# Moving weight packing, a slot table and an exponential to other steps of a two-layer graph kernel

## The chip, the core and the metric

The kernel runs on one core of a Trainium2 chip. A core has a matrix engine (TensorE, PE in the profile; PEld is its weight load), a vector engine (VectorE, DVE), a scalar engine for activations (ScalarE, ACT), a general engine (GpSimd, POOL) and a queue engine that only starts transfers (SyncE, SP). Each works through its own instructions in order, and they wait for each other by semaphores. Sixteen DMA engines carry the transfers that SP, ACT and POOL start. The metric is the device time of one execution in microseconds, and of several executions the median.

## The reference

Two layers follow each other on x of 2708 rows and 256 columns, with a 0/1 matrix adj of 2708 by 2708. Each layer is an attention over the graph and a mixture of eight experts of which each row uses two.

```python
# layer 0
x = x + elu(softmax(where(adj > 0, q @ k.T / 16, -9e15)) @ v)      # q, k, v from layernorm(x)
x = x + ffn0(layernorm(x))      # top 2 of 8 experts, 256 -> 1024 -> 256, gelu, own layer norm
# layer 1
x = x + softmax(where(A > 0, s_src + s_dst + b, -1e9)) @ H         # H = layernorm(x) @ W_fc + b_fc
x = x + ffn1(layernorm(x))      # top 2 of 8 experts, 256 -> 512 -> 256, gelu
```

## The kernel before

**Stages.** Attention of layer 0, expert stage of layer 0, attention of layer 1, expert stage of layer 1, and a last sum. The change touches the first of these and, through what it takes away from it, the second.

**Attention of layer 0** (`layer0_attention`). The queries are cut into six blocks: five of 512 rows and a last one of 148 (`BLOCKS`; `last` is 5). For each block a loop runs over 22 tiles of 128 keys (`for k in range(NT)`); a pass through it is called a key step here. A key step multiplies keys with queries (`scores`, L568), takes the exponential on ScalarE (L580), multiplies by the mask on VectorE (L583), and, three steps later (`LAG`), multiplies the result with the values (`attend`, L632). Score results lie in two buffers of PSUM (`ps_s`). In block 0 the rows of x are also normalised and turned (`prepare`), four tiles ahead of their use.

**Masks.** The mask of a block is made in the block before it (`masks_of`, one step per key step from key 2), from 1 MB pieces of adj that SP loads into three buffers. The first block's own mask is made beside it. When a block is done, its mask is stored in DRAM (L741), since layer 1 uses it again; six entries at the end of the background list load the masks back into SBUF (`mT<-neighbours`).

**Background list.** `background` is a list of transfers that depend on nothing in the kernel: 2 fills of scratch rows (`disp<-nobody`), then 32 pieces that copy expert weights of layer 0 from their places in DRAM into one packed row per partition (`pack_weights`, pieces of 512 KB and a few small ones, L1067 to L1085), then 16 entries of two 256 KB pieces each for layer 1, and, from the end of the attention on, the 6 loads of masks. One entry is taken in every second key step of the attention, from key 11 of block 1 on, and none in the last block: 39 in all. What remains is taken in the expert stage, one in every second slot (L1616).

**What follows a block.** When a block's last key has been attended, its up to four accumulators are copied out (`evict`, L657), and each tile of 128 rows gets a generator `finish`. `line` starts these generators with a gap of so many key steps (3, in the last block 4) and moves every running one by a step in each key step (`line.step()`), from block 1 on. A step ends at a `yield`. The first step of `finish` divides by the row sum and takes the negative part (L644) and its exponential (L645); the second forms the elu and adds x; then `experts0.route` normalises the row, finds the two best experts (L1243 to L1259), takes an exponential for their weights (L1261), counts with two small matmuls (L1264, L1265) and scatters the row by an indirect transfer into the rows of its experts (L1282). The first 16 tiles find the logits by dot products on VectorE (L261), the others by a matmul (L1232).

**The slot table.** The expert stage works in slots of 128 rows of one expert. Weights of a slot lie in one of four ring buffers. The first 24 slots are worked out during the last block, from the first 16 tiles, by `place(0, 24)`: a small matmul for the counts (L1303), and some twenty VectorE instructions (L1305 to L1394), with four `yield`s in between. `begin_steps` puts a `yield` before it, then fetches rows for three slots (`fetch_rows`, SP: four transfers of 32 KB and one small one each, L1465 and L1471), then weights for three slots (`fetch_weights`, POOL, L1446), each with a `yield`. The ring's first three buffers are filled by a guess beforehand (L1441, three loads of 2182 KB).

**Order.** SP's order is the order of the program in the whole kernel. In blocks 0 to 4 the other engines' instructions are ordered by a planner when the kernel is built, with the program's order as priority. From the last block on the order of PE, ACT and DVE is also the program's (`order0`); POOL's isn't.

**Expert stage of layer 0** (`slots`). A slot takes 48 recorded matmuls in two parts (`up`, L1533, and `down`, L1549) with a gelu between them (L1541); the next slot's rows are turned and scaled on VectorE (L1506, L1512), which reads the slot's weights from its ring buffer. Two `line.step()` per slot finish the last tiles' routes. When they are done, or at slot 21, the remaining slots are placed.

Of the kernel before, what the change touches and what calls it, by code (L numbers as in the profile page):

```python
# [77 lines left out]
LAG = 3  # L78
# [26 lines left out]
def adj_ffn_kernel(ctx: ExitStack, tc: tile.TileContext, a: dict, out: bass.AP):  # L105
# [208 lines left out]
    def over_sum(raw, r, n, total, alone):  # L314

        z = small.tile([P, 2], F32, name="z")
        nc.vector.tensor_scalar(alone, raw[:r, n : n + 1], 0.0, None, ALU.is_equal)
        nc.vector.scalar_tensor_tensor(
            z[:r, 0:1], alone, float(N), raw[:r, n : n + 1], op0=ALU.mult, op1=ALU.add
        )  # L320
        nc.vector.reciprocal(z[:r, 1:2], z[:r, 0:1])
        nc.vector.scalar_tensor_tensor(
            raw[:r, :n], total[:r], alone, raw[:r, :n], op0=ALU.mult, op1=ALU.add
        )
        return z[:r, 1:2]
# [47 lines left out]
    def layer0_attention(line):  # L373
        with ExitStack() as scope, ExitStack() as until_last:

            last = len(BLOCKS) - 1
# [18 lines left out]
            def load_x(t):  # L395
                xin[t] = rows0.tile([P, D], F32, name="xin", bufs=9)
                nc.sync.dma_start(xin[t][: ROWS[t]], of_tile(a["x"], t))
# [60 lines left out]
            def mask_of(b):  # L458
                mT = of_block(b, "mT", [P, MASKS[b].width], FP8, bufs=3)
                nc.gpsimd.memset(MASKS[b].of_key(mT, NT - 1).bitcast(F32), 0.0)  # L460
                return mT

            def norm_begin(t):
                r, src = ROWS[t], xin.pop(t)
                return t, src, norm_stats(src[:r], r)

            def norm_end(t, src, stats):
                r, (mean, factor, *_) = ROWS[t], stats
                xn = rows.tile([P, D], F32, name="xn", bufs=4)
                normed(xn[:r], src[:r], mean, factor)  # L470
                return xn

            def prepare(t, xn):
                r = ROWS[t]
                at = xnT[:, :, t * P : t * P + r]
                if t < NT - 1:
                    to_columns(at, xn[:r], r)
                else:
                    tail_columns(x_tail, xn)
                    nc.vector.tensor_copy(at, x_tail[:, :, :r])  # L480
                    r, at = P, x_tail
                nc.vector.tensor_reduce(
                    sums_of[:, :, t], xnT[:, :, t * P : t * P + ROWS[t]], AX.X, ALU.add
                )
                ps = misc.tile([P, GROUP, P], F32, name="misc").rearrange("p g n -> p (g n)")
                for c in range(DC):
                    nc.tensor.matmul(
                        ps[:r, :D], at[:, c, :], wv[:, c, :],
                        start=(c == 0), stop=(c == DC - 1),
                    )  # L490
                nc.scalar.copy(v[:r, t, :D], ps[:r, :D])
# [145 lines left out]
            def finish(t, raw, total):  # L637
                r, xr = ROWS[t], xin.pop(t)
                rinv = over_sum(raw, r, D, total, alone[:r, t : t + 1])
                nc.vector.scalar_tensor_tensor(  # L640
                    raw[:r, :D], raw[:r, :D], rinv, bv_b[:r], op0=ALU.mult, op1=ALU.add
                )
                neg = rows0.tile([P, D], F32, name="neg", bufs=2)
                nc.vector.tensor_scalar(neg[:r], raw[:r, :D], 0.0, None, ALU.min)  # L644
                nc.scalar.activation(neg[:r], neg[:r], AF.Exp)  # L645
                yield
                nc.vector.scalar_tensor_tensor(
                    neg[:r], neg[:r], -1.0, raw[:r, :D], op0=ALU.add, op1=ALU.max
                )
                x1 = rows0.tile([P, D], F32, name="x1")  # L650
                nc.vector.tensor_add(x1[:r], neg[:r], xr[:r])
                yield from experts0.route(t, x1)
# [14 lines left out]
            for b, (b0, nb, ts_) in enumerate(BLOCKS):  # L667
                later_mask = iter(())
                if b == last:
                    line.gap = GROUP  # L670
                    order0.enter_context(
                        tc.manual_schedule(engines={
                            mybir.EngineType.PE,
                            mybir.EngineType.Activation,
                            mybir.EngineType.DVE,
                        })
                    )
                if b + 1 < len(BLOCKS):
                    mT_next = mask_of(b + 1)
                    later_mask = masks_of(b + 1, mT_next)  # L680
                for k in range(NT):
                    if b == 0:
                        if k + 9 < NT:
                            load_x(k + 9)
                        next(first_mask, None)
                        if k + 4 < NT:
                            prepare(k + 4, norm_end(*norm_begin(k + 4)))

                    j = k - (2 if b == last else NT - 1 - GROUP)
                    if 0 <= j < len(ts_):  # L690
                        load_x(ts_[j])
                    if k == (0 if b == last else GROUP):
                        apart_adj = load_apart(b)
                    if k == NT - 8:
                        apart = compare_apart(*apart_adj)
                    late.append((b, k, scores(b, k, g, apart, mT)))
                    if len(late) > LAG:
                        b_, k_, p = late.pop(0)
                        if k_ == 0:
                            accs = [  # L700
                                ps_acc.tile([P, D + 1], F32, name="acc") for _ in BLOCKS[b_][2]
                            ]
                        attend(b_, k_, p, accs)
                        if k_ == NT - 1:
                            evict(b_, accs, total)
                    if b == 1 and k % GROUP == 0:
                        next(folding, None)
                    if b == 0 and k == NT - 1:
                        sums = wide.tile([P, DC], F32, name="sums", bufs=1)
                        nc.vector.tensor_reduce(sums, sums_of, AX.X, ALU.add)  # L710
                        total = all_sum(wide, sums, wv, D, "total0")
                    if b == 0 and k == NT - 4:
                        raw = wide.tile([P, BN // QUARTER, P], I32, name="adj", bufs=3)
                        raw = raw.rearrange("p n e -> p (n e)").bitcast(F32)
                        nc.sync.dma_start(
                            raw, a["L0_ffn_Wr"].rearrange("d e -> (d e)").partition_broadcast(P)
                        )
                        gate_rows(raw)
                    if k == NT - 6 and b + 1 < len(BLOCKS):
                        g_next = queries(b + 1)  # L720
                    if k >= 2:
                        next(later_mask, None)
                    if background and k % 2 == 1 and b < last and (b > 1 or (b == 1 and k > 10)):
                        background.pop(0)()
                    if b > 0:
                        line.step()
                    if b == last and k == LAG:
                        until_last.close()
                    if b == last and k == LAG + 2:
                        n = FULL_AFTER[experts0.early]  # L730
                        guess0 = experts0.open(
                            [i * (n // RING) * E // (n + GROUP) for i in range(AHEAD)] + [-1]
                        )
                        for _ in range(AHEAD):
                            next(guess0)
                        begin0 = experts0.begin()
                        for _ in range(6):
                            next(begin0)
                    if b == last and k in (LAG + 7, LAG + 11, LAG + 15):
                        next(begin0)  # L740
                nc.sync.dma_start(neighbours[b][:], mT)  # L741
                if b < last:
                    for _ in later_mask:
                        pass
                    g, mT = g_next, mT_next
# [903 lines left out]
    background = []  # L1649
# [92 lines left out]
```

## Time and profile before

Three executions took 1217.05 us in the median (1210.39 to 1219.58). The profiled execution took 1209.07 us; its span, from first to last instruction, is 1206.8 us, with a mean granted TensorE clock of 0.981.

| engine | busy us | share of the span | instructions |
|---|---|---|---|
| VectorE | 621.0 | 51% | 2389 |
| ScalarE | 422.9 | 35% | 1234 |
| GpSimd | 419.9 | 35% | 524 |

| stretch | us |
|---|---|
| blocks 1 to 4 of the first attention | 81.5, 82.7, 79.6, 78.5 |
| last block (148 queries) | 54.2 |
| first expert stage | 332.9 |

Block starts are the starts of the first score matmul (L568) of a block. The page cuts the span into 40 slices of 30 us and gives the busy share of each engine in tenths, then the granted clock and the mean share of the DMA engines. A long busy share says which engine is in demand; where that engine idles, the instruction behind the gap says what it waited for. In the timeline each line is a start, a duration, the engine, the source line, the operation, what it writes and reads, and in brackets how long the engine had been idle and what ended that.

### The profile page before, as it was taken

What the parts mean: (1) busy time and instruction counts of PE and PEld (TensorE: products, weight loads), DVE (VectorE), ACT (ScalarE), POOL (GpSimd) and SP (SyncE); (2) the same over time, 40 slices, a digit from 0 to 9 for tenths busy, and PEclk for the clock granted to TensorE, in tenths of its full rate; (3) what the DMA queues carried; (4) which work ended last, traced back from release to release, by engine and by line L of the source; (5) the groups of instructions that cost most, each with busy time, mean ns of one, the idle gap of its engine ahead of it and who ended that gap; (6) DMA issues with size and microseconds to landing.
All of it is one profiled execution on the core that took longest, in us unless ns stands there. A gap on an engine that the chain in (4) does not pass through costs nothing. (4 is left out here: it accounts for less than half of the span.)

```text
span 1206.8 us, 20877 instructions
## 1 busy us (share of the span) xinstructions
PE 1131.4 (94%) x6416; PEld 914.3 (76%) x6416; DVE 621.0 (51%) x2389; ACT 422.9 (35%) x1234; POOL 419.9 (35%) x524
## 2 busy tenths in 40 slices
PE   8989999999999998899999999998999998999990
PEld 5666666656666664699989989996999977899880
DVE  5465992865856747652222222224866777322214
ACT  3222221212122121443333323333776657544430
POOL 3011220120220303244333234433745557655540
PEclk9999999999999998999999999999999999999995
DMA  9293864976683389367868968634001527655557
GB/s 221 42 195 91 195 158 124 237 177 136 163 214 101 97 205 364 79 169 183 212 182 234 375 172 252 175 105 105 1 2 54 202 61 209 180 157 145 147 167 284
DMA packets 200717, 198.16 MB, mean 164 GB/s; under 512 B 92363, under 2 KB 183972, under 8 KB 194328
## 3 DMA queue, kind: packets, MB, share of 16 engines
q1 hardware_dynamic: 173530, 117.14, 39.6%
q0 software_dynamic: 26176, 76.85, 20.1%
q10 hardware_dynamic: 894, 2.77, 0.6%
q8 instruction: 53, 0.87, 0.3%
q14 instruction: 64, 0.52, 0.1%
HBM read 260.37 MB, written 66.15 MB: 271 GB/s over the span
## 5 line engine op out<-in xcount | busy, mean ns | idle before, releaser
L1533 PEld LDWEIGHTS mm<-xe,ring 128*128 128x128 f32 x2192 | 259.1, 193 | 25.4 <-DVE xe L1512 7.8
L1533 PE MATMUL mm<-xe,ring 128*128 128x128 f32 x2192 | 262.9, 277 | 16.3 <-DMA ring<-L_ffn_packed,weight_row 7.7
L1549 PE MATMUL acc<-ring,hT 128*128 128x256 f32 x1096 | 253.8, 382 | 0.7 <-ACT hT L1541 0.7
L1541 ACT ACTIVATE hT<-mm,ring 128x128 f32<-128x128 f32 x548 | 155.8, 369 | 273.2 <-PE mm L1533 139.4
L1549 PEld LDWEIGHTS acc<-ring,hT 128*128 128x128 f32 x1096 | 202.8, 192 | 25.0 <-ACT hT L1541 0.9
L632 PEld LDWEIGHTS acc<-v,p 128*128 128x128 f32 (+1 forms) x880 | 160.0, 190 | 63.4 <-issue 37.5
L568 PE MATMUL s<-g,xnT 128*128 128x512 f32 x420 | 202.3, 601 | 3.3 <-ACT p L580 3.3
L632 PE MATMUL acc<-v,p 128*128 128x257 f32 (+1 forms) x880 | 204.2, 384 | 0.6 <-DVE p L583 0.6
L1555 DVE SCALAR_TENSOR_TENSOR y<-acc,who,bias 128x256 f32<-128x256 f32 x92 | 44.4, 482 | 267.3 <-PE acc L1549 264.6
L277 POOL TENSOR_TENSOR ln_rs<-ln_rs,minus_half 128x2 f32<-128x2 f32 x88 | 66.1, 754 | 233.0 <-DVE ln_rs L273 210.0
L1282 POOL DMA_INDIRECT disp<-row,to x88 | 89.0, 1012 | 153.8 <-DVE to L1279 33.5
L1446 POOL DMA_INDIRECT ring<-L_ffn_packed,weight_row x92 | 97.5, 1059 | 107.7 <-PE acc L1549 68.5
L901 PE MATMUL acc<-parts,m 128*128 128x266 f32 x924 | 127.6, 296 | 0.0
L580 ACT ACTIVATE p<-s 128x512 f32<-128x512 f32 x105 | 62.0, 594 | 179.0 <-PE s L568 149.9
L901 PEld LDWEIGHTS acc<-parts,m 128*128 128x128 f32 x924 | 118.3, 187 | 4.4 <-ACT raw L928 0.9
L568 PEld LDWEIGHTS s<-g,xnT 128*128 128x128 f32 x420 | 77.3, 191 | 56.1 <-issue 48.2
L1568 POOL DMA_INDIRECT xd<-y,who x45 | 70.9, 1575 | 140.2 <-issue 71.3
L583 DVE SCALAR_TENSOR_TENSOR p<-p,mT 128x512 f32<-128x512 f32 x100 | 72.3, 725 | 58.3 <-ACT p L580 58.1
L868 ACT CAST m<-mT 128x512 fp32r<-128x512 fp8e4 (+4 forms) x168 | 72.2, 475 | 11.0 <-PE acc L901 7.6
L1512 DVE TENSOR_SCALAR xe<-xe_raw,ring 128x128 f32<-128x128 f32 x90 | 28.0, 360 | 65.7 <-DMA ring<-L_ffn_packed,weight_row 64.6
L1561 POOL DMA_INDIRECT xd<-y,who x47 | 46.9, 998 | 26.0 <-DVE y L1555 13.3
L261 DVE SCALAR_TENSOR_TENSOR row<-x,wr_rows 128x256 f32<-128x256 f32 x128 | 53.0, 416 | 0.3
(257 smaller groups left out, 1051.5 us busy)
## 6 DMA issues: line engine op xcount, KB each, us to landing
adj<-in_adj_dram SPq DMA_DIRECT2D x100, 256.0 KB
L_ffn_packed<-in_L_ffn_W_dram SPq DMA_DIRECT2D x32, 512.0 KB
xg<-disp SPq DMA_DIRECT2D x368, 32.0 KB
L_ffn_packed<-in_L_ffn_W_dram SPq DMA_DIRECT2D x32, 256.0 KB
neighbours<-mT SPq DMA_DIRECT2D x5, 1408.0 KB
mT<-neighbours SPq DMA_DIRECT2D x5, 1408.0 KB
ring<-L_ffn_packed SPq DMA_DIRECT2D x3, 2182.0 KB
xin<-in_x_dram SPq DMA_DIRECT2D x42, 128.0 KB
```

The costliest lines, as they stand in the source:

```text
L277: nc.gpsimd.tensor_tensor(rs[:r, 1], rs[:r, 0], minus_half[:r], ALU.pow)
L568: nc.tensor.matmul(ps[:kr, :nb], xnT[:, c, k0 : k0 + kr], g[:, c, :nb], start=(c == 0), stop=(c == DC - 1 and k < KEYS),)
L583: nc.vector.scalar_tensor_tensor(p, p, LARGEST, mask, op0=ALU.min, op1=ALU.mult)
L632: nc.tensor.matmul(accs[j][:r], p[keys, q0 : q0 + r], v[keys, k, :], start=(k == 0), stop=(k == NT - 1),)
L868: nc.scalar.copy(m[:, : q1 - q0], MASKS[b].of_key(mTs[b], k)[:, q0 - b * BN : q1 - b * BN],)
L901: nc.tensor.matmul(acc[:r], masks[t], parts[:, k, i], start=(k == 0 and i == 0), stop=False,)
L1282: nc.gpsimd.indirect_dma_start(disp[:], bass.IndirectOffsetOnAxis(ap=to[:r, j : j + 1], axis=0), rows2[:r, j], None,)
L1446: nc.gpsimd.indirect_dma_start(w, None, packed[:], bass.IndirectOffsetOnAxis(ap=self.weight_row[:, s : s + 1], axis=0), bounds_check=E * P ...
L1533: nc.tensor.matmul(ps[:, i, :], w[:, c * hidden + f * P : c * hidden + (f + 1) * P], xe[:, c, :], start=(c == 0), stop=(c == DC - 1),)
L1541: nc.scalar.activation(hT[:, f, :], ps[:, i, :], AF.Gelu, bias=w[:, b1 + f : b1 + f + 1])
L1549: nc.tensor.matmul(ps, hT[:, f, :], w[:, w2 + f * D : w2 + (f + 1) * D], start=(f == 0), stop=(f == hc - 1),)
L1568: start = nc.gpsimd.indirect_dma_start(xd[:], at, y, None, bounds_check=N - 1, oob_is_err=False, compute_op=ALU.add)
```

## The change

Three places in `layer0_attention`:

```diff
@@ finish @@
                 nc.vector.tensor_scalar(neg[:r], raw[:r, :D], 0.0, None, ALU.min)
+                yield
                 nc.scalar.activation(neg[:r], neg[:r], AF.Exp)
                 yield
@@ the loop over keys @@
-                    if background and k % 2 == 1 and b < last and (b > 1 or (b == 1 and k > 10)):
+                    if background and k % 2 == 1 and b < last and (b > 0 or k > 8):
                         background.pop(0)()
...
                         begin0 = experts0.begin()
-                        for _ in range(6):
-                            next(begin0)
-                    if b == last and k in (LAG + 7, LAG + 11, LAG + 15):
+                    if b == last and LAG + 2 <= k < LAG + 8:
+                        next(begin0)
+                    if b == last and k in (LAG + 9, LAG + 12, LAG + 15):
                         next(begin0)
```

The exponential of the negative part becomes a step of its own, one key step behind the instruction that forms the negative part; all later steps of a tile move by one. The background list is drawn on from key 9 of block 0 instead of key 11 of block 1: 51 places in the attention instead of 39, for 50 entries. In the last block the six steps that work out the slot table and fetch its rows, all taken at key 5 before, are taken one each at keys 5 to 10 (the first of them only reaches the first `yield`), and the three weight fetches at keys 12, 15 and 18 instead of 10, 14 and 18. No computation is added or left out.

## The prediction

> **What bounds the kernel now.** I read the page's shares first, then busy time by stretch (the six attention blocks by the starts of their score matmuls, and the first expert stage), then TensorE's waits in each stretch, and last the order in time around the long waits.
>
> ```profile
> PE 1131.4 (94%) x6416; PEld 914.3 (76%) x6416; DVE 621.0 (51%) x2389; ACT 422.9 (35%) x1234; POOL 419.9 (35%) x524
> ...
> 284.80:364.40 79.60, 78.48 (x302) 50.43 (x301) 53.43 (x225) 17.10 (x38) 13.24 (x19) 1.00 0.79 191
> 364.40:442.90 78.50, 77.50 (x306) 50.85 (x305) 52.47 (x219) 16.97 (x38) 16.27 (x25) 1.00 0.53 127
> 442.90:497.10 54.20, 46.48 (x242) 27.80 (x240) 35.13 (x152) 10.90 (x42) 14.61 (x26) 0.94 0.78 272
> 497.10:830.00 332.90, 325.68 (x2204) 304.03 (x2205) 96.43 (x306) 110.36 (x373) 122.02 (x96) 1.00 0.69 190
> ```
>
> Columns: stretch, length, then busy us of PE, weight load, DVE, ACT, POOL, the granted clock, DMA share, GB/s. TensorE leads everywhere, so a microsecond is won only where it idles or runs at a lower clock. Blocks 3 and 4 idle 1.1 and 1.0 us. The last block idles 7.7 of 54.2 us at a mean clock of 0.94: the change's main place. The first expert stage idles 7.2 us in 333.
>
> ```profile
> 458.92 0.61 PE L632 MATMUL acc<-v,p_last 128*20 128x257 f32 x2
> ...
> 460.60 0.18 DVE L1369 CAST token_row<-row 128x24 int32<-128x24 f32 x1
> ...
> 461.57 0.30 DVE L583 SCALAR_TENSOR_TENSOR p_last<-p_last,mT_last 128x148 f32<-128x148 f32 x1
> ...
> 463.60 0.42 ACT L645 ACTIVATE neg<-neg 128x256 f32<-128x256 f32 x1 [7.26 <-DVE neg L644]
> 463.92 0.46 ACT L580 ACTIVATE p_last<-s 128x148 f32<-128x148 f32 x2
> ...
> 464.25 1.35 PE L568 MATMUL s<-g_last,xnT 128*128 128x148 f32 x4 [4.72 <-ACT p_last L580]
> ```
>
> This is the long wait. The slot table's DVE chain (L1305 to L1394) runs from 457.04 to 461.65 in one piece; behind it come a mask product and the next tile's first part, ending in L644 at 463.56; ScalarE holds L645 at its head until then, and two score exponentials behind it; TensorE needs one of them to free a score buffer. It stands 4.72 us.
>
> ```profile
> 256.90 3.55 PE L568 MATMUL s<-g,xnT 128*128 128x512 f32 x4 [2.20 <-ACT p L580]
> ...
> 324.32 1.99 PE L568 MATMUL s<-g,xnT 128*128 128x512 f32 x4 [1.12 <-ACT p L580]
> ...
> PE mm L1533 <- DVE xe L1512: 5.7, 4, 2.6
> ...
> 698.72 0.60 DVE L1512 TENSOR_SCALAR xe<-xe_raw,ring 128x128 f32<-128x128 f32 x2 [7.98 <-DMA ring<-L_ffn_packed,weight_row]
> 699.12 3.87 PE L1533 MATMUL mm<-xe,ring 128*128 128x128 f32 x32 [2.62 <-DVE xe L1512]
> ```
>
> The other losses: two ScalarE-caused waits in blocks 2 and 3, and in the first expert stage four waits (1.11 at 509, 1.43 at 611, 0.53 at 682, 2.62 at 699; 5.7 in all), three of them on expert weights still in transfer.
>
> **What the Trainium skill says.** "TensorE: Matmul & The Clock Gate", What's actually happening: an idle array drops to half clock after about 3.4 us and needs as long a busy stretch to recover. The trace agrees on half speed (four 128x148 score matmuls take 1.35 us behind the stall, 0.75 to 0.77 elsewhere), but shows it already after 2.20 us (3.55 us against 1.88). "DMA: Bandwidth & Descriptors", Issuing engines are not separate DMA queues: transfers from SP and POOL share 16 engines and interleave. That agrees with weight fetches (POOL) arriving late just when SP's mask loads ran: 375 GB/s in that slice of the page. "Perfetto Trace Analysis", Sequencer Loop: an instruction waits for its semaphores in its engine's order; L645 above is that case.
>
> **Part 1: the table in five key steps.** Nothing is removed: 4.6 us of DVE work (457.04 to 461.65) falls into about 0.2, 1.6, 0.75, 1.45 and 0.55 us at keys 6 to 10 of the last block. PE's key step takes 1.7 us (472.07, 473.73, 475.47). Worth at most: the stall 4.72, and the slow clock behind it, where key steps took 3.19 and 2.59 us instead of 1.7 and 2.0: 2.1. Together 6.8.
>
> But DVE is next. I lined up its work by key from the durations of its rows: mask product 0.33; a tile's first part 1.8 (461.80 to 463.56), second 1.8 (465.42 to 467.23), normalising 1.1, top two 1.05, last part 0.9. Keys 5 to 12 then ask about 20 us of DVE against 14 us of PE, and the backlog that the three keys between score and product allow is used up near key 14. From there PE is paced by the exponentials behind tile 19's L644 (mine: about 478 instead of 481.35) and by its normalised row (about 484 instead of 486.6). I put the last score group at 484.5 instead of 488.97: **4.5 us**. Ends: 2 if the DVE pace is worse by one tile part, 6.8 if it hides.
>
> The row fetches move from key 5 to key 10 with the table: three times five SP transfers (L1465, L1471), now behind one more tile's store. SP waits there for token_row (about 466 instead of 460.8). Cover: three ring loads of 2182 KB issued at 457.04 block SP anyway: four row transfers from 465.06 took 18.32 us, to 483.4. First use is near 492, so nothing; without that cover some 6 us later, which would still land before 492. The weight fetches (POOL, 1.06 us each to issue) at keys 12, 15, 18 instead of 10, 14, 18 get their table some 8 us later, near 469.5; the fourth slot needs its weights only 21 us after the stage begins: nothing.
>
> **Part 2: the exponential a step later.** One ScalarE instruction of 0.42 us a tile, 22 of them, not removed. ScalarE idled 53.3 us before it on L644, but PE lost only the 1.12 us at 324 (and the stall above): **1.1 us**. The 2.20 at 256.90, plus 1.85 at half clock (3.55+2.08 against 1.88+1.90), belongs to another exponential (L1261, behind L1249), which isn't moved; I leave it. Each route ends a step later; at three steps between tiles DVE sees the same work, otherwise interleaved. In blocks 1 to 4 the order isn't written out by hand, so this is unknown: from +4.05 (the L1261 event goes) to -4.05 (another one appears) per block. I take nought. In the first expert stage DVE's 3.41 us wait before L647 at 504.54 goes, as its instruction now stands behind the next slot's input; with it the 1.11 at 509.
>
> **Part 3: packing from key 9 of block 0.** 7 entries come into block 0 (two fills of 129 KB, five of 512 KB) and 5 into block 1; all others move forward by 12, so all 50 are out before the last block. SP issues some 11 more transfers of 0.5 to 0.6 us in block 0, about 6 us. Cover: own masks and input rows are issued by key 12, packing of weights begins at key 13; DMA is 0.48, 0.73, 0.38 and 0.00 busy in the ten-us slices from 80 to 120. The gate's 1 MB load (SP at 104.29) is read by DVE only at 120.4. Block 1 gets the density of blocks 2 and 3, which idle little. Nothing; without the cover, up to 4 us at the start of block 1 (one half-clock event).
>
> The first expert stage loses eleven entries (SP at 513 to 651), and six mask loads move from slots 23 to 33 (SP at 666 to 742) to slots 1 to 11. The waits at 611, 682 and 699 sat under this traffic; without it, slots after 745 show none. Worth 4.6. Mask loads now meet the weight fetches of the first slots (249 GB/s at 540 to 555, where a packing entry is replaced by 1408 KB): I give back 2.2 of 4.6, close to the largest single wait, and take **2.4**; bounds -3 (all 5.7 again with more) to 4.6.
>
> **Sum.** 4.5 + 1.1 + 1.1 + 2.4 = 9.1 us. The profiled execution took 1209.07 us (span 1206.8 and 2.27 around it), so 1200 of its kind. It lies 8 us below the median of the runs; subtracted from 1217.05 it gives **1208 us**.
>
> **Rivals.** (a) *More is won*: DVE's backlog hides (6.8), the expert stage keeps 4.6 and the event at 256.9 goes (4.05): 6.8+2.2+4.6+4.05 = 17.7, 1199 us. For: ScalarE no longer waits at every tile. Against: 29.45 us DVE busy in the 38 us from 452 to 490. 30%. (b) *Nothing is won*: DVE's total is unchanged, so spreading only splits the stall, and the mask loads give their waits back: gains of 2 at most, 1215. 15%. (c) *Slower*: in blocks 1 to 4 the later exponential lengthens each route, DVE (13 to 14 of 15 us in stretches of blocks 2 and 3) delays L1249 or L644 more, and the event of 256.90 repeats, at 2.20 + 1.85 = 4.05 each. From three new ones the gain is gone; two in each of four blocks (32.4) less 9.1 give 1240, five give 1217 + 20.3 - 9.1 = 1228. Against: ScalarE's slack grows by a step. 12%. A change that doesn't do what it says is excluded by the code.
>
> **Numbers.** My forecast 43%. Its own range is 1202 to 1213; with (a), (b) and part of (c) 1197 to 1221. A change within 1% (12.2 us) is about what cannot be told from none: the three runs spread over 9.2 us. Faster by over 1%: all of (a) and a little of the forecast, 0.33; slower: most of (c), 0.11; same: 0.56.
>
> **What would show it.** Part 1 is right if the table's groups lie between other DVE work, the 4.72 disappears, the clock of the last block returns to 1.0, and its length falls to about 49.7. It is wrong if a wait of over 3 us on a ScalarE exponential stands in keys 9 to 18. Part 2: waits of L645 on L644 fall from 53.3 to under 20 us. Part 3: block 0 and 1 as long as before, no packing after the last block begins, no wait near the turn of the slots' second half; wrong if the first expert stage is longer. The forecast as a whole falls if blocks 1 to 4 (322.3 us) change by over 5 us.

## The result and the profile after

The change made the kernel slower: 1226.11 us in the median of seven executions (1223.01 to 1230.34) against 1217.05 (1210.39 to 1219.58), also of seven, a ratio of 1.0085 with a 95% interval of 1.0057 to 1.0114 (the two medians alone give 1.0074). The profiled execution of the changed kernel took 1230.34 us (span 1228.6), the longest of its seven; that of the kernel before took 1209.07 us and lies 8 us below its median. So the two traces differ by 21 us where the medians differ by 9, and the readings below rest on differences that come back in further traces.

In the changed kernel lines from 645 on carry a number higher by one: the exponential is L646, the mask store L742, the packing L1068 to L1086, the ring loads L1442, the row fetches L1466.

The busy times of the page, then the stretches from the first score matmul of the last block to the first matmul of a slot, and from there to the matmuls that bridge to the next stage (L1632; L1631 before):

```profile
PE 1137.7 (93%) x6416; PEld 916.2 (75%) x6416; DVE 619.9 (50%) x2389; ACT 427.6 (35%) x1238; POOL 421.3 (34%) x524
```

```profile
445.66:516.46 70.80, 50.63 (x241) 29.39 (x242) 41.93 (x193) 11.47 (x44) 17.46 (x29) 0.86 0.80 243
516.46:838.46 322.00, 320.20 (x2179) 300.69 (x2180) 95.90 (x305) 115.43 (x377) 121.22 (x95) 0.99 0.64 181
```

Shares and busy times hardly moved. The last block did: 70.8 us instead of 54.2, TensorE idle for 20 of them and at a clock of 0.86. The expert stage, bounded in the same way, is shorter, 322.0 instead of 325.3. What TensorE waited for in the changed last block (sum, times, longest), and the three long waits in order of time:

```profile
PE misc L294 <- DVE xn L281: 8.0, 2, 6.3
PE misc L1265 <- DVE sel L1260: 4.6, 2, 4.0
PE acc L632 <- DVE p_last L583: 4.5, 1, 4.5
```

```profile
462.32 0.17 PE L1265 MATMUL misc<-sel,before 128*128 128x8 bf16 x1 [4.01 <-DVE sel L1260]
...
463.00 1.34 PE L568 MATMUL s<-g_last,xnT 128*128 128x148 f32 x4
...
472.50 0.69 PE L294 MATMUL misc<-ident,xn 128*128 128x128 f32 x2 [6.33 <-DVE xn L281]
472.98 1.19 PE L568 MATMUL s<-g_last,xnT 128*128 128x148 f32 x4
...
476.91 1.14 PE L632 MATMUL acc<-v,p_last 128*128 128x257 f32 x4
477.98 0.77 PE L568 MATMUL s<-g_last,xnT 128*128 128x148 f32 x4
483.23 2.20 PE L632 MATMUL acc<-v,p_last 128*128 128x257 f32 x4 [4.48 <-DVE p_last L583]
```

The wait of 4.72 us on a score exponential is gone. In its place stand three others, each with slowed matmuls behind it: four score matmuls take 1.34 and 1.19 us instead of 0.77, and four value matmuls 2.20 us instead of 1.14. VectorE's timeline of the same time tells what the second and third hang on:

```profile
469.50 0.42 DVE L652 TENSOR_TENSOR x<-neg,xin 128x256 f32<-128x256 f32 x1 [6.29 <-DMA xin<-in_x_dram]
...
482.79 0.17 DVE L1306 COPY n_e<-misc 128x8 f32<-128x8 f32 x1 [8.24 <-DMA neighbours<-mT]
482.87 0.30 DVE L583 SCALAR_TENSOR_TENSOR p_last<-p_last,mT_last 128x148 f32<-128x148 f32 x1
```

One waits for a row load of x, the other for the store of block 4's mask: the table's first tile `n_e` lies in memory that the mask held, and a mask product that TensorE needs is queued behind it. Both transfers come late out of SP. SP's queue in the changed kernel, and then before, around the turn from block 4 to the last block:

```profile
443.44 0.35 SPq L422 DMA_DIRECT2D adj<-in_adj_dram  x1
443.84 1.15 SPq L1068 DMA_DIRECT2D L_ffn_packed<-in_L_ffn_W_dram  x2
...
463.08 0.59 SPq L397 DMA_DIRECT2D xin<-in_x_dram  x1
463.71 1.13 SPq L1068 DMA_DIRECT2D L_ffn_packed<-in_L_ffn_W_dram  x2
464.89 1.21 SPq L397 DMA_DIRECT2D xin<-in_x_dram  x2
...
470.37 0.61 SPq L1082 DMA_DIRECT2D L_ffn_packed<-in_L_ffn_b_dram  x1
471.02 0.59 SPq L397 DMA_DIRECT2D xin<-in_x_dram  x1
471.65 0.43 SPq L742 DMA_DIRECT2D neighbours<-mT  x1
...
482.79 1.28 SPq L1442 DMA_DIRECT2D ring<-L_ffn_packed  x3
```

```profile
447.64 1.15 SPq L1067 DMA_DIRECT2D L_ffn_packed<-in_L_ffn_W_dram  x2
448.89 0.54 SPq L741 DMA_DIRECT2D neighbours<-mT  x1
...
451.31 2.73 SPq L397 DMA_DIRECT2D xin<-in_x_dram  x2
...
457.04 2.19 SPq L1441 DMA_DIRECT2D ring<-L_ffn_packed  x3
```

Before, the last packing entry started at 447.64. In the changed kernel SP is through with the last loads of adj for the last block's mask only at 443.8, and behind them stand eight of block 4's ten packing entries, 4 MB from DRAM to DRAM, started one after another until 470.98, 25 us into the last block. Call it the pile. It isn't made of more entries in block 4, which had eleven before, but of entries that leave late. SP's own waits around block 4 say why it comes so late (the changed kernel, then before):

```profile
SPq L418 <- POOL adj L410: 25.0, 2, 18.5
SPq L418 <- POOL row L1205: 13.6, 1, 13.6
```

```profile
SPq L418 <- POOL adj L410: 18.0, 1, 18.0
SPq L418 <- POOL row L1204: 9.7, 1, 9.7
```

SP stands at a load of adj until GpSimd has cleared the buffer, and GpSimd until VectorE has read it. In VectorE's timelines, one of the last transposes of block 4's own mask is at 386.86 before and at 411.62 in the changed kernel:

```profile
386.86 0.63 DVE L437 STREAM_TRANSPOSE mT<-m_rows 128x128 int32<-128x128 int32 x2
```

```profile
411.62 0.64 DVE L437 STREAM_TRANSPOSE mT<-m_rows 128x128 int32<-128x128 int32 x2
```

### The profile page after: what moved, and what is told of

It is laid out like the page before. It is cut to its first block, busy times and chain, and to the rows that moved or that the text cites. A ratio compares the mean times of both kernels' runs of the same rounds, so it can differ in the third digit from the quotient of the medians.

```text
span 1228.6 us, 20867 instructions
## 1 busy us (share of the span) xinstructions
PE 1137.7 (93%) x6416; PEld 916.2 (75%) x6416; DVE 619.9 (50%) x2389; ACT 427.6 (35%) x1238; POOL 421.3 (34%) x524
## 5 line engine op out<-in xcount | busy, mean ns | idle before, releaser
L277 POOL TENSOR_TENSOR ln_rs<-ln_rs,minus_half 128x2 f32<-128x2 f32 x88 | 66.5, 757 | 272.1 <-DVE ln_rs L273 247.0
L1283 POOL DMA_INDIRECT disp<-row,to x88 | 89.6, 1018 | 136.3 <-DVE to L1280 42.6
L568 PEld LDWEIGHTS s<-g,xnT 128*128 128x128 f32 x420 | 77.5, 190 | 53.9 <-issue 48.7
L583 DVE SCALAR_TENSOR_TENSOR p<-p,mT 128x512 f32<-128x512 f32 x100 | 70.8, 709 | 79.6 <-ACT p L580 79.6
L1569 POOL DMA_INDIRECT xd<-y,who x45 | 71.6, 1592 | 112.4 <-DVE xe L1513 55.8
L261 DVE SCALAR_TENSOR_TENSOR row<-x,wr_rows 128x256 f32<-128x256 f32 x128 | 52.6, 415 | 0.5
```

Of the source, the lines that this page charges most:

```text
L277: nc.gpsimd.tensor_tensor(rs[:r, 1], rs[:r, 0], minus_half[:r], ALU.pow)
L568: nc.tensor.matmul(ps[:kr, :nb], xnT[:, c, k0 : k0 + kr], g[:, c, :nb], start=(c == 0), stop=(c == DC - 1 and k < KEYS),)
L583: nc.vector.scalar_tensor_tensor(p, p, LARGEST, mask, op0=ALU.min, op1=ALU.mult)
L1283: nc.gpsimd.indirect_dma_start(disp[:], bass.IndirectOffsetOnAxis(ap=to[:r, j : j + 1], axis=0), rows2[:r, j], None,)
L1569: start = nc.gpsimd.indirect_dma_start(xd[:], at, y, None, bounds_check=N - 1, oob_is_err=False, compute_op=ALU.add)
```

## The experiments

**The theories.** T1: the earlier packing does it, by the pile. T2: the later exponential does it, by putting routes and masks later in the plan, and the packing only rides along. T3: the table in steps does it, since its counts then wait for SP. Variants of T1 (a to e) are told where they come in.

**The table of all runs.** Ratios are to the kernel before, run beside each; stages are those of one profiled execution. "Blocks 1–4" runs from the small matmul L303 at the turn of block 0 to the first score of the last block; "rest" is everything behind the first expert stage.

| kernel | ratio (95%) | blocks 1–4 | last block | expert stage | rest |
|---|---|---|---|---|---|
| before | 1 | 321.3 | 54.2 | 325.3 | 384.3 |
| changed | 1.0085 (1.0057–1.0114) | 323.9 | 70.8 | 322.0 | 390.1 |
| table_only | 1.0035 (1.0018–1.0051) | 321.4 | 56.7 | 329.8 | 384.7 |
| exp_only | 0.9965 (0.9945–0.9984) | 316.6 | 54.9 | 327.7 | 382.6 |
| pack_only | 1.0148 (1.0110–1.0186) | 324.1 | 77.4 | 321.4 | 384.6 |
| table_exp | 0.9934 (0.9913–0.9954) | 316.6 | 51.3 | 331.3 | 384.9 |
| exp_pack | 1.0117 (1.0085–1.0150) | 323.9 | 73.9 | 319.7 | 382.7 |
| no_pack_block4 | 1.0055 (1.0040–1.0070) | 324.0 | 56.1 | 327.0 | 384.8 |
| pack_block4_early | 1.0030 (1.0015–1.0046) | 324.0 | 55.8 | 323.6 | 384.4 |
| pack_block0_only | 1.0041 (1.0024–1.0059) | 327.1 | 55.2 | 332.1 | 385.3 |
| pack_block1 | 0.9996 (0.9978–1.0014) | 316.5 | 63.1 | 326.8 | 380.4 |
| pack_block1_stop | 0.9948 (0.9931–0.9966) | 316.5 | 53.9 | 326.4 | 383.8 |
| rows_early | 1.0086 (1.0055–1.0117) | 324.0 | 69.0 | 319.5 | 386.9 |
| store_apart | 1.0171 (1.0136–1.0206) | 324.0 | 77.4 | 321.1 | 387.5 |
| rows_store | 1.0166 (1.0131–1.0201) | 323.9 | 74.9 | 323.5 | 385.4 |
| stop_rows_store | 0.9944 (0.9923–0.9965) | 316.4 | 53.1 | 328.6 | 385.9 |
| table3_exp | 0.9961 (0.9944–0.9977) | 316.5 | 53.1 | 331.8 | 382.2 |

Medians of the kernel before beside these ratios are 1211.9 to 1212.6 us (1217.05 beside the changed kernel), so 0.1% is 1.2 us. "Rest" isn't touched by any edit; it spreads over 380 to 388 us, and the 390.1 of the changed kernel's one trace is not counted as an effect.

### Which of the three parts

Each part alone on the kernel before, and the change without one part. The three edits are the hunks of the change:

```diff
+                yield                                                        # exp
-                    if background and k % 2 == 1 and b < last and (b > 1 or (b == 1 and k > 10)):  # pack
+                    if background and k % 2 == 1 and b < last and (b > 0 or k > 8):
-                        for _ in range(6):                                   # table
-                            next(begin0)
+                    if b == last and LAG + 2 <= k < LAG + 8:
+                        next(begin0)
```

> Only the table in five key steps, packing and exponential as before. T1 (the earlier packing does the harm, by a burst of packing in SP's queue at the start of the last block) and T2 (the later exponential does it, by changing the planned order in blocks 1 to 4): 2 to 7 us faster than before, the 4.72 us wait on the last scores' exponential gone, last block 48 to 52 us against 54.2. T3 (the spread table itself does it, because the table's count of entries then waits for SP): 8 us or more slower, last block over 60 us.

> Only the exponential a step later. T1: within 3 us of before, SP's packing ends before the last block begins. T2: 6 to 14 us slower, a tile's route falls into the last block, masks formed some 20 us later in block 4, and the last block is over 62 us. T3: within 3 us.

> Only the packing from key 9 of the first block. T1: 7 to 14 us slower, ten packing entries of layer 1 issued within 30 us around the start of the last block, the last input rows and the last mask's store behind them, two TensorE waits of over 4 us there, last block over 62 us. T2 and T3: within 4 us of before, either way, last block 52 to 56 us.

> The changed kernel with the packing begun as before (block 1, key 11). T1: 3 to 9 us faster than before, some 12 to 18 us faster than the changed kernel; last block 48 to 52 us. T2: 5 to 12 us slower than before, as the changed kernel. T3: slower by 8 or more, as with the table alone.

> The changed kernel with the table at once, as before: what is left is the later exponential and the earlier packing. If the parts add up as in the runs with one part: 1.0148 - 0.0035 = 1.011 of before, between 1.009 and 1.014, last block 73 to 79 us. If the table in steps gives nothing when the packing is early: as the changed kernel, 1.007 to 1.010.

Measured: the packing alone costs 1.48% (18 us), more than any theory had said; on top of the exponential 1.52 (1.0117 against 0.9965), on top of both others 1.51. The total grows by as much whatever stands beside it, so T1 holds, though its 7 to 14 us were too few, and T2 falls: the later exponential alone is *faster* by 0.35% (4.2 us, a little more than the 3 us either way that T1 had allowed), with blocks 1 to 4 shorter by 4.7 us. By stretch the two don't add up: packing costs blocks 1 to 4 2.8 us without the later exponential (321.3 to 324.1) and 7.3 with it (316.6 to 323.9), and the last block 23.2 and 19.0 us. Beside the earlier packing, the exponential's gain in blocks 1 to 4 is gone (324.1 and 323.9). TensorE's waits from 215 to 330 us, before and with the exponential alone, show where that gain comes from:

```profile
PE s L568 <- ACT p L580: 3.3, 2, 2.2
```

```profile
PE s L568 <- ACT p L580: 0.2, 1, 0.2
```

Not only the 1.12 us at 324 went, but the 2.20 us at 256.90 too, and with it the half clock behind it. Where the T1 line said that SP's packing ends before the last block, it was wrong: it ends at 446.0 with the block starting at 438.8, as before (448.8 and 442.9); that alone does no harm.

The table alone missed every line: it is slower by 0.35%, not faster, and far from T3's 8 us. Its last block holds a wait that was not foreseen (TensorE, then VectorE):

```profile
500.65 9.15 PE L1533 MATMUL mm<-xe,ring 128*128 128x128 f32 x64 [6.52 <-DVE xe L1512]
```

```profile
499.62 0.45 DVE L1506 STREAM_TRANSPOSE xe_raw<-xg 128x256 f32<-128x256 f32 x1 [5.56 <-DMA xg<-disp]
```

The scores are done earlier, and then the first slot waits for its rows. With the exponential a step later the same table gains 0.31% (0.9934 against 0.9965), with the packing as well 0.32% (1.0085 against 1.0117, where 1.011 had been foreseen by adding; these two intervals overlap), and the rows are in time (a wait of 0.53 us for them in table_exp). Why they were late in the one kernel only isn't settled; the landing of these transfers isn't in the trace.

### Where the packing hurts

All four have the later exponential and the table in steps; only the condition on the background list differs.

```diff
-if background and k % 2 == 1 and b < last and (b > 0 or k > 8):
+if background and k % 2 == 1 and b < last and (b > 0 or k > 8) and b < last - 1:             # no_pack_block4
+if background and k % 2 == 1 and b < last and (b > 0 or k > 8) and (b < last - 1 or k < 9):  # pack_block4_early
+if background and k % 2 == 1 and b < last and (b > 1 or (b == 0 and k > 8)):                 # pack_block0_only
+if background and k % 2 == 1 and b < last and b > 0:                                         # pack_block1
```

> The changed kernel, packing from key 9 of block 0, but no packing drawn in block 4, so ten entries are left to the first expert stage. The masks lag as in the changed kernel (the mask of block 4 is formed until about 410 us). T1a (the lag does harm only because a pile of packing then stands in SP's queue ahead of the last input rows and the last mask's store): the two long waits of the last block go, last block under 56 us, total 0.990 to 1.000 of before. T1b (the lagging masks themselves do the harm): last block stays over 62 us, total 1.005 to 1.015 of before.

> The changed kernel, packing drawn in block 4 only until key 7 (four entries), six left to the first expert stage. T1a: four entries still meet the lagging mask loads, but the pile at the turn of the block is some half as long: last block 54 to 62 us, total 0.996 to 1.004. T1b: as the changed kernel, 1.005 to 1.012.

> The changed kernel with seven packing entries in block 0 and none in block 1, the rest from block 2 on. T1c (packing at one entry per two keys in block after block leaves no room in which the masks catch up; a block without it lets them): the mask of block 4 is done near 386 us again, last block under 54 us, total 0.990 to 0.998 of before. T1d (the entries in block 0 do the harm by themselves, being ahead of the first mask loads of block 1): 1.004 or more, last block over 60 us.

> The changed kernel with packing from key 1 of block 1: five entries earlier than before, seven fewer than in the change, none in block 0. T1c: the harm grows with the lag, so between: mask of block 4 formed until some 395 us, last block 54 to 64 us, total 0.995 to 1.006. T1d: as the table and exponential alone, 0.990 to 0.995.

Without packing in block 4, or with four entries early in it, the last block is 56 us: the pile is worth some 15 us. The stretches and TensorE's waits of the last block without packing in block 4:

```profile
445.57:501.70 56.13, 46.89 (x242) 28.19 (x243) 40.83 (x193) 11.56 (x44) 17.76 (x29) 0.94 0.62 218
```

```profile
PE misc L1265 <- DVE sel L1260: 5.2, 2, 5.0
PE misc L294 <- DVE xn L281: 2.4, 2, 1.7
```

The waits of 6.3 and 4.5 are gone. The wait of 4 to 5 us on a late tile's route (L1260) stays, so it isn't the pile's (in pack_block1 it is 0.5 us). With four entries the total is in T1a's range (1.0030). Without any it is 1.0055, where T1a had said at most 1.000 and T1b 1.005 to 1.015. A second cost lies elsewhere: with the later exponential, blocks 1 to 4 take 324.0 instead of 316.6 us in every kernel that packs in blocks 0 and 1, with the pile or without. It is made of small waits: from 100 us to the first score of the last block TensorE's add up to 8.4 us in the changed kernel and to 2.6 with the exponential alone, most of the 8.4 (6.9) on VectorE.

This second cost comes with the entries in block 0. With them alone (seven, none in block 1), blocks 1 to 4 take 327.1, with two waits on ScalarE of 2.8 and 2.4 us; without them, from block 1 on, 316.5, as if nothing had been moved. T1d's total came true for the entries in block 0 (1.0041), though not its last block (55.2 us, where over 60 was said), and T1c's ranges for packing from block 1 on (0.9996 and 63.1 us). What costs in blocks 1 to 4 isn't the lag of the masks as such. Block 4's mask is finished some 32 us into its block in pack_block1 and some 22 us in pack_block0_only, as with the exponential alone, and yet blocks 1 to 4 take 316.5 us in the first and 327.1 in the second. The lag harms later: it holds SP at the loads of adj, and with packing late in block 4 the pile follows. The first mask piece that VectorE makes in block 1 (it is block 2's), before and with the packing alone:

```profile
140.87 0.76 DVE L431 TENSOR_SCALAR m_rows<-adj 128x512 fp8e4<-128x512 int32 x2
```

```profile
156.53 0.95 DVE L431 TENSOR_SCALAR m_rows<-adj 128x512 fp8e4<-128x512 int32 x2
```

No idle time stands in brackets in the second line: VectorE wasn't waiting for adj, it had other work in front of it. The order itself differs: this piece comes after three of the row dot products (L261) in the eight kernels without packing in block 0, and after 16 or 17 in the nine with it, the same nine whose blocks 1 to 4 take 323.9 us or more. In blocks 0 to 4 that order is the planner's, so the packing in block 0 changed the plan, not only the transfers. That the planner counts the packing's transfers in front of the mask loads fits, but was not tried.

### The version without the pile

```diff
-if background and k % 2 == 1 and b < last and (b > 0 or k > 8):                    # pack_block1_stop
+if background and k % 2 == 1 and b < last and b > 0 and (b < last - 1 or k < 13):
-                    if b == last and LAG + 2 <= k < LAG + 8:       # table3_exp (packing as before)
+                    if b == last and LAG + 2 <= k < LAG + 5:
+                        next(begin0)
                         next(begin0)
```

> The changed kernel with packing from key 1 of block 1, none in block 0, and none in block 4 after key 11; four entries are left to the first expert stage. T1a with T1c (small lag, no pile at the turn of the block): blocks 0 to 4 until 438 to 440 us, last block 51 to 55 us instead of 63.1, total 0.987 to 0.994 of before, the fastest of all. Rival (the lag of one third that remains costs as much by itself as the pile): last block over 58 us, total 0.996 or more.

> Packing as before, exponential a step later, and the table in three key steps of two parts each instead of five, so that the first slots' rows are asked for three keys (some 5 us) earlier. If the late row loads are what takes back part of the table's gain: first expert stage 327 to 330 us against 331.3 with five steps, last block 50 to 53 us, total 0.989 to 0.993 of before. If finer steps are what helps: last block 52 to 55 us, total 0.993 to 0.998.

Packing from key 1 of block 1 without the last five places of block 4 leaves eleven entries to the expert stage, as before (the "four" in the expectation is a miscount). The last block falls from 63.1 to 53.9 us, the total by 0.5%: so the pile, not the small lag (some 32 us into block 4 in both), cost there. It beats the kernel before, but not table_exp (0.9948 and 0.9934, the intervals overlap). The table in three steps is no better than in five (0.9961; last block 53.1 against 51.3, expert stage the same), so asking for the rows earlier gives nothing here. That fits the line on finer steps, though the two intervals just overlap.

### Is it the order in SP's queue?

```diff
-                    j = k - (2 if b == last else NT - 1 - GROUP)
+                    j = k - (2 if b == last else 6 if b == last - 1 else NT - 1 - GROUP)   # rows_early, rows_store
-                nc.sync.dma_start(neighbours[b][:], mT)
+                store = nc.scalar if b == last - 1 else nc.sync                            # store_apart, rows_store
+                store.dma_start(neighbours[b][:].bitcast(F32), mT.bitcast(F32))
```

`stop_rows_store` is pack_block1_stop with both edits.

> The changed kernel, with the four x rows of block 4's tiles loaded from key 6 of block 4 instead of key 16, so they stand ahead of most of the packing in SP's queue; packing, masks and the mask store are as in the change. T1a (what stops TensorE is that input rows and the mask store stand behind the pile in SP's queue): the 6.3 us wait on a tile's normalised row goes, the wait on the mask product behind the table's count (4.5 us, it depends on the mask store, which stays behind the pile) remains or grows, last block 61 to 66 us instead of 70.8, total 1.000 to 1.006 of before. T1e (the pile's traffic itself is what holds TensorE up, wherever the rows stand): last block stays at 68 us or more, total 1.007 to 1.011.

> The changed kernel, with the store of block 4's mask started from ScalarE's queue instead of SP's, so that it isn't behind the packing; the x rows stay behind it. T1a' (two things are behind the pile, and the later one sets the end): the wait of the table's count on the mask store is gone or under 2 us, the wait on a tile's x rows (6.3 us) stays; last block 62 to 68 us, total 1.000 to 1.006. T1e (traffic): last block 68 us or more.

> The changed kernel with both: x rows loaded from key 6 of block 4, and the mask store started from ScalarE's queue. All packing stays where the change puts it. T1a': neither wait is left, last block 54 to 60 us (a late route of 4 to 5 us stays, as with no packing in block 4), total 0.995 to 1.003 of before. T1e: the packing's traffic holds TensorE up all the same, last block over 65 us, total 1.006 or more.

> Packing from key 1 of block 1, none in block 4 after key 11, with early x rows and the mask store from ScalarE's queue. T1a': the 4.5 us of waits on normalised rows in the last block go in part, last block 50 to 53 us, total 0.990 to 0.995 of before. If these waits had other causes: as without the two moves, 0.993 to 0.997.

With the rows ahead of the pile, the wait for them goes and the next one takes its place. Counted from the first score of the last block it ends at 35.6 us, where it ended at 37.6 without the edit (TensorE, rows_early):

```profile
481.72 2.20 PE L632 MATMUL acc<-v,p_last 128*128 128x257 f32 x4 [8.65 <-DVE p_last L583]
```

With the store alone out of the pile (store_apart), the wait on a row of x stays and grows to 13.3 us. With both out, both waits are gone, and a third stands there (GpSimd and TensorE, rows_store, whose lines are one higher again):

```profile
483.77 0.75 POOL L277 TENSOR_TENSOR ln_rs<-ln_rs,minus_half 128x2 f32<-128x2 f32 x1
...
498.46 1.11 POOL L1448 DMA_INDIRECT ring<-L_ffn_packed,weight_row  x1 [13.69 <-DMA ring<-L_ffn_packed]
...
504.70 0.75 POOL L277 TENSOR_TENSOR ln_rs<-ln_rs,minus_half 128x2 f32<-128x2 f32 x1
```

```profile
506.28 0.69 PE L294 MATMUL misc<-ident,xn 128*128 128x128 f32 x2 [13.50 <-DVE xn L281]
```

The ring loads are behind the pile too (started at 484.39); a weight fetch on GpSimd waits for one of them, and the next norm factor (L277) stands behind that fetch in GpSimd's order. T1a' had named two of three, so its numbers failed (74.9 us, not 54 to 60), and in all three kernels the last block lies where T1e had put it (69.0, 77.4 and 74.9 us), as do the totals that it gave. The test isn't clean: with the store on ScalarE's queue, SP waited 7.6 us for the store's transfer at a load of adj, and the pile began at 450.88 instead of 443.84. "The Trainium skill", page "DMA: Bandwidth & Descriptors", Issuing engines are not separate DMA queues, says that a start from another engine saves only time on the starting sequencer. The runs show no gain from it either (1.0171 against 1.0085), but as the edit also delayed the pile they don't test the statement. In `stop_rows_store`, without the pile, the two moves change nothing that can be told: 0.9944 and 0.9948, a last block of 53.1 and 53.9 us, waits on normalised rows of 4.9 and 4.5 us, so these have another cause.

Over all traces the last block's length follows how far into it SP still starts packing: up to 11 us into it the last block takes 51 to 57 us, with 19 us (pack_block1) 63.1, with 25 to 34 us 69 to 77. Shown is that the pile must not be there at this time; whether its place in SP's order or its traffic counts for more stays open.

## Why the prediction was wrong

**What failed: the packing in the attention, costed at "Nothing; without the cover, up to 4 us".** Beside the other two parts it cost 7.3 us in blocks 1 to 4 (316.6 to 323.9) and 19.5 in the last block (51.3 to 70.8). The step that failed is "all 50 are out before the last block": they are taken from the list before it, but SP starts the last of them 25 us into it (470.37, first score at 445.66). Even before, the last one left at 447.64, 4.7 us into the last block. Two sentences carried the zero. "Block 1 gets the density of blocks 2 and 3, which idle little" looked at TensorE's idle time, and not at how late the masks of blocks 2 and 3 already were: before, the mask of block 2 is finished 5 us ahead of its block, those of blocks 3 and 4 only 10 and 23 us into theirs (294.8 and 387.5, starts 284.8 and 364.4), so the masks lose ground from block to block already. And the cover named for block 0 was about transfers and DMA share, while the order in which VectorE takes the mask work is a plan in which the packing has a part, as the moved dot products show; why the plan comes out so is open. What packing in block 4 is queued ahead of in SP's order (rows, mask store, ring loads) was listed for the table's row fetches, but never for part 3: all fifty entries were moved, and the working looked only at blocks 0 and 1 where the first of them landed.

**Part 1, 4.5 us.** With the exponential it is 0.31%, with the packing as well 0.32%, some 4 us: the size was right, as far as these intervals tell, and so was the wait that went. "The row fetches … nothing" held there; with the table alone it failed, by the 6.52 us wait of the first slot.

**Part 2, 1.1 + 1.1 us.** Measured alone 0.35%, 4.2 us. The term that was mis-sized is the event of 256.90, "I leave it": it went. It hung on L1261's exponential, not the moved one, but in the planner's new order it doesn't come. The working's bound (4.05, a gain) holds the value. ScalarE's waits on L644 fell to 36.2 us only in the changed kernel, not under 20, and that didn't matter.

**Part 3 in the expert stage, 2.4 us.** Direction right; measured are 9.3 us between table_exp and the changed kernel and 3.9 between before and packing alone. TensorE's waits on the slot input, in the changed kernel and in table_exp:

```profile
PE mm L1534 <- DVE xe L1513: 2.3, 2, 1.6
```

```profile
PE mm L1534 <- DVE xe L1513: 8.4, 6, 2.7
```

That the mask loads gave back less than assumed fits this, but isn't shown: every kernel with no entries left for the stage also has a long last block, and with ten or eleven left the stage takes anything from 325.3 to 332.1 us.

**The sum.** From table_exp to the changed kernel: 7.3 + 19.5 - 9.3 = 17.5 us, against 18 from the ratios. With 8 us won by the first two parts, 10 are lost; the prediction had 9 won.

**The rivals.** Rival (c) had the sign, but not the mechanism: no event of 256.90 came back, the later exponential removed one. Two of rival (a)'s gains came (the event of 256.90; the expert stage's, with the doubt above); its third, 6.8 us for the table, did not. What would show it: the criterion "blocks 1 to 4 change by over 5 us" stayed silent (+2.6), because the packing took back what the exponential gains there alone. The signs for single parts told at once: the last block was to fall to 49.7 us and took 70.8, and packing was not to go on after it began.

## What to carry to other kernels

A list of "free" background transfers isn't free where the queue that starts them also carries work with a date: when it is drawn on earlier, look at the place where the *last* entries now stand, and at what is queued behind them there. Where one in-order queue waits for a buffer (here SP at a load of adj), everything due behind it leaves as one pile, so a stop a few steps ahead of a stage's turn (53.9 us against 63.1) is worth more than an earlier start. Test parts of a change one by one: two of three here won 0.66%, and the third hid it.

## What the runs showed of the hardware

A wait for a buffer holds the engine that starts the transfers, not the DMA engines. SP stood 18.5 us at one load of adj in the changed block 4 (418.7 to 437.3), and the packing behind it, which depends on nothing, wasn't started either; GpSimd's scatters (L1283) went out meanwhile, at 424.80 and 431.78, and the DMA share of 430 to 440 us was 0.19. The skill's page "DMA: Bandwidth & Descriptors", Anatomy of one DMA — SWDGE (gpsimd) path, says that DMA engines don't wait for semaphores and that the issuing sequencer does so before dispatch. It says so of GpSimd's path; this trace agrees for SP. The stretches of ten us after it in the changed kernel:

```profile
460.00:470.00 10.00, 3.38 (x11) 1.76 (x10) 3.33 (x20) 0.59 (x3) 2.01 (x2) 0.60 0.87 227
470.00:480.00 10.00, 6.25 (x26) 3.87 (x26) 3.71 (x14) 1.26 (x4) 1.00 (x3) 0.71 0.92 229
...
490.00:500.00 10.00, 7.84 (x44) 4.70 (x43) 8.62 (x47) 2.08 (x9) 5.05 (x5) 1.00 1.01 415
```

With the packing from DRAM to DRAM and the mask store running, the DMA engines are 0.87 to 0.92 busy for 227 to 229 GB/s; with the loads of weights into SBUF (490 to 500) they are full at 415. Divided by their shares the rows give 249 to 261 and 411 GB/s, so by an estimate from them a packed megabyte takes the room of about 1.6 loaded ones; the mask store and GpSimd's transfers are in these stretches too.
